# A graph-attention kernel whose second layer is normalized after its product instead of before

## The chip, the cores and the metric

The kernel runs on one core of a Trainium2 chip. The metric is the time of one execution on the device in microseconds; lower is better. A profile of one execution shows what each engine of the core did: TensorE (PE, with its weight loads as PEld), VectorE (DVE), ScalarE (ACT), GpSimd (POOL) and SyncE (SP), and the transfers (DMA) that SP and POOL issue.

## The reference

Two graph-attention layers are applied to 32 independent graphs of 512 nodes, and their result is added to the input. For each graph:

```python
h = maximum(layernorm(x), 0)                       # x: [512, 512]
h = elu(gat_layer(h, mask, W1, as1, ad1, b1))      # 4 heads of 256, concatenated: [512, 1024]
h = gat_layer(h, mask, W2, as2, ad2, b2)           # 1 head of 512
out = x + h

def gat_layer(x, mask, W, a_src, a_dst, bias):
    xl = x @ W                                     # per head
    asrc, adst = xl . a_src, xl . a_dst            # one score per node and head
    e = leaky_relu(asrc[s] + adst[d], 0.2)         # [source, destination]
    e = where(mask, e, -1e9)
    attn = softmax(e, over sources s)
    return sum over s of attn[s, d] * xl[s] + bias
```

`mask` is the adjacency matrix with the diagonal set. All is in f32.

## The kernel before, in words

One batch is one graph. `B` is 32; rows are taken in `NT` = 4 blocks of 128. Every large product is a Strassen-like scheme of seven half-size products (numbered 1 to 7), whose operands are sums and differences made on VectorE beforehand, and whose results are gathered in PSUM banks and evicted by ScalarE or VectorE. Per batch there are four products: the first projection (`project1`, 55 matmuls of 258 columns), the first layer's weighted sums (`gather1`, 56 of 256 columns, in two halves of two heads), the second projection (`project2`, 56 of 257: 256 features and one score column, twice), and the second layer's weighted sums (`gather2`, 28 of 256).

The main loop (L1702 to L1759) interleaves three batches. In its iteration `i` TensorE does the first half of `gather1` of batch `i+1`, 19 steps of `project1` of batch `i+2`, the second half of `gather1` of `i+1`, the rest of `project1` of `i+2`, then `gather2` of batch `i`, then `project2` of `i+1`. Beside this, the input of batch `i+3` is loaded, normalized, and turned by `norm_turn`: ScalarE splits the f32 words into 16-bit halves, a DMA transpose on SP turns them (`x<-adj` in the profile), and ScalarE merges the halves into `ht`.

The softmax weights of one head are made by the class `Soft` in two passes. The first pass (`first`) has destinations on the partitions: for each block of 128 destinations ScalarE takes the leaky ReLU of the scores (`l<-as,z`), VectorE applies the mask and takes the least negated value (`l<-l,mt`, with the result in column block 0 of `low`), and ScalarE exponentiates and sums (`l<-l,low`, sum in column block 1 of `low`). The logarithm of that sum is subtracted from the extreme, so that `low` holds minus (maximum + log sum). `spread` broadcasts these per-destination values to all partitions by way of DRAM (`drr<-rr`, `rr<-drr`). The second pass (`second`) has sources on the partitions: VectorE makes the leaky ReLU shifted by the broadcast values, a POOL transfer adds the mask (`p<-dm`), and ScalarE exponentiates. The weights `p` come out normalized.

`gather2` multiplies `p` with the projected features `xl2`. `residual(i)` loads the four row blocks of x into four `t` tiles before it; the function `put` inside `gather2` adds every one of the 14 results from PSUM to its half of a row block on VectorE (`t<-mm,t`), and when a row block is complete SP stores it (`out_dram<-t`). The tiles `t` are also the operands `t<-p` of `gather1`.

Nothing in the order of the work outside TensorE is written out by hand. All operations are collected as jobs with an engine, an estimated cost, reads and writes. The order of TensorE's jobs is that of the program. For the other engines a planner (`Program.order`, `Run.go`) simulates the queues with its estimated costs, and `Program.better` looks for holes of TensorE in its own model; for each it tries up to `TRIES` changes of the other engines' priorities, and keeps those that help. The order found is then emitted; every engine executes its list in order.

Of the kernel before, what the change touches and what calls it, by code (L numbers as in the profile page):

```python
# [11 lines left out]
F32 = mybir.dt.float32  # L12
# [4 lines left out]
OP = mybir.AluOpType  # L17
# [186 lines left out]
class Program:  # L204
# [224 lines left out]
    MARK, SIGHT, TRIES, BACK = 20, 80, 100, 5.0  # L429
# [83 lines left out]
def tile_gat(  # L513
# [66 lines left out]
    half = sbuf.tile([P, NT], F32, name="half")  # L580
# [10 lines left out]
    c2 = sbuf.tile([P, 2], F32, name="c2")  # L591
    cols2 = sbuf.tile([P, 2, 2], F32, name="cols2")
# [11 lines left out]
    xs = slots("x", NT, [P, D])  # L604
# [5 lines left out]
    ts_ = slots("t", 4, [P, N])  # L610
# [341 lines left out]
    class Soft:  # L952


        def __init__(self, b, layer, scores):
            self.b, self.layer, self.scores = b, layer, scores
            self.g = 2 if layer == 1 else 1
            self.z, self.asr, self.low, self.rr, self.p = {}, {}, {}, {}, {}
# [46 lines left out]
        def first(self, h, parts=((0, NT),)):  # L1005
# [9 lines left out]
            for d0, d1 in parts:  # L1015
                for d in range(d0, d1):
                    lk, e = ls.take()
                    act(
# [3 lines left out]
                    e3 = e.rearrange("p (t r) -> p t r", r=P)  # L1022
# [13 lines left out]
                act(0.25, tot, tot, low[:, 1, d0:d1], low[:, 1, d0:d1], AF.Ln)  # L1036
                dve(
                    TINY, lo + tot, lo, nc.vector.tensor_sub,
                    low[:, 0, d0:d1], low[:, 0, d0:d1], low[:, 1, d0:d1],
                )  # L1040
# [129 lines left out]
    def sevens(left, right, rkeys, put, kh, units, width, order, seeds={}):  # L1170
# [3 lines left out]
        for u, n in order:  # L1174
            m = units[u][0]
            acc, first = ACC[n], n in (1, 2, 5)
# [16 lines left out]
            put(n, units[u], bk, ps)  # L1193
# [360 lines left out]
    def sums2(b, soft, place=None, keys=None):  # L1554
# [4 lines left out]
        v = x2(b)  # L1559
        b11, b12, b21, b22 = (  # L1560
            (
                v[:, 2 * r : 2 * r + 2, c * W2H : c * W2H + M],
# [5 lines left out]
            (t.rearrange("p (k f) -> p k f", f=M), [k]) for k, t in (xs.take() for _ in range(3))  # L1568
# [13 lines left out]
    def gather2(b, soft, blocks, order=NEAR):  # L1582
        left, right = blocks
        xr = XR.pop(b)
        upper = [2, 2]

        def put(n, u, bk, ps):
            r, c = BLOCK[n - 1]
            d = 2 * r + u[0]
            place, xk, xt = xr[d]  # L1590
            to = xt[:, c * M : (c + 1) * M]
            dve(ADD, [bk, xk + (c,)], [xk + (c,)], nc.vector.tensor_tensor, to, ps, to, op=OP.add)

            upper[u[0]] -= n in (2, 3)
            if n == 4 or r == 0 and upper[u[0]] == 0:
                upper[u[0]] = -1
                dma(0.65, [xk, xk + (0,), xk + (1,)], (), out[b, d * P : (d + 1) * P, :], xt)
                place.give(xk)
# [3 lines left out]
            [(0,), (1,)], M, order,  # L1602
# [31 lines left out]
    def second_layer(b):  # L1634
        s = Soft(b, 2, scores_2(b))
        s.columns(0)

# [64 lines left out]
    for i in range(B - 1):  # L1702
# [37 lines left out]
        if i < B - 3:  # L1740
            residual(i)
# [59 lines left out]
```

## Time and profile before

| | |
|---|---|
| Median of 3 runs | 2754.67 us (2753.43 to 2755.41) |
| Profiled execution, its own time | 2758.68 us |
| Its span, first to last instruction | 2756.9 us |
| Mean granted TensorE clock | 0.999 |
| Matmul instructions (two for each f32 matmul) | 12490 |
| VectorE instructions counted as busy | 6744 |
| ScalarE instructions counted as busy | 4871 |
| Issues of the mask transfer p<-dm | 314, median 4.9 us to landing |
| Loads of x into t tiles | 124 |
| Stores of t tiles | 124 |

The lines of the profile give for each engine its busy time, that time's share of the span, and its instructions. Groups of instructions are named as output<-inputs by the program's names, without buffer numbers. Since all operations are emitted by helpers, the line numbers are those of the helpers: L646 is ScalarE's `act`, L649 VectorE's `dve`, L652 SP's `dma`, L657 POOL's `accumulate`, L663 TensorE's `pe`; L932 is the transpose of x. Times in a timeline are counted from the start of the span. Matmuls overlap, so that one that takes 379 ns follows the one before it by about 216.

### The profile page before, as it was taken

What the parts mean: (1) busy time and instruction counts of PE and PEld (TensorE: products, weight loads), DVE (VectorE), ACT (ScalarE), POOL (GpSimd) and SP (SyncE); (2) the same over time, 40 slices, a digit from 0 to 9 for tenths busy, and PEclk for the clock granted to TensorE, in tenths of its full rate; (3) what the DMA queues carried; (4) which work ended last, traced back from release to release, by engine and by line L of the source; (5) the groups of instructions that cost most, each with busy time, mean ns of one, the idle gap of its engine ahead of it and who ended that gap; (6) DMA issues with size and microseconds to landing.
All of it is one profiled execution on the core that took longest, in us unless ns stands there. A gap on an engine that the chain in (4) does not pass through costs nothing.

```text
span 2756.9 us, 41901 instructions
## 1 busy us (share of the span) xinstructions
PE 2732.9 (99%) x12490; PEld 2367.0 (86%) x12490; DVE 2595.0 (94%) x6744; ACT 2281.9 (83%) x4871; POOL 326.5 (12%) x356
## 2 busy tenths in 40 slices
PE   7999999999999999999999999999999999999999
PEld 6688888888888888888888888888888888888887
DVE  8999999999999999999999999999999999999996
ACT  5978898888888888988889887888888898888973
POOL 0111110101111011111011110111111111101110
PEclk9999999999999999999999999999999999999999
DMA  8756866667676677666776666766666766777663
GB/s 225 182 162 181 206 177 173 182 182 194 174 193 176 177 184 206 179 168 183 187 207 173 182 176 183 191 188 182 178 182 180 213 173 172 185 183 199 169 169 108
DMA packets 375863, 502.10 MB, mean 182 GB/s; under 512 B 222804, under 2 KB 227668, under 8 KB 375636
## 3 DMA queue, kind: packets, MB, share of 16 engines
q1 hardware_dynamic: 329844, 332.68, 43.3%
q0 software_dynamic: 45792, 166.74, 24.7%
q8 instruction: 100, 1.64, 0.2%
q14 instruction: 127, 1.04, 0.1%
HBM read 316.41 MB, written 51.31 MB: 133 GB/s over the span
## 4 chain that ended last, share of the span: by engine, by line
PE 97%; DMA 1%; ACT 1%; DVE 0%; SPq 0%; issue 0%; ACTq 0%
PE mm L663 97%; DMA x<-adj 0%; DMA w_sb<-dm 0%; ACT l L646 0%; DMA w_sb<-in_L_gnn_W_dram 0%; DMA as<-das 0%; DMA das<-as 0%; SPq L652 0%; DVE h L649 0%; ACT x L646 0%; DVE hs L649 0%; ACT ht L646 0%; DVE w_sb L649 0%; ACT w_sb L646 0%; DVE xl L649 0%
## 5 line engine op out<-in xcount | busy, mean ns | idle before, releaser
L663 PE MATMUL mm<-w_sb,hs 128*128 128x257 f32 (+2 forms) x3032 | 696.4, 380 | 2.2 <-ACT xl L646 1.6
L663 PEld LDWEIGHTS mm<-w_sb,hs 128*128 128x128 f32 x3032 | 575.3, 190 | 87.7 <-ACT xl L646 2.4
L657 POOL DMA_DIRECT2D p<-dm x314 | 274.3, 878 | 2330.5 <-DVE p L649 1312.6
L646 ACT ACTIVATE l<-l,low 128x512 f32<-128x512 f32 x640 | 458.2, 719 | 23.1 <-DVE low L649 20.6
L663 PE MATMUL mm<-w_sb,h 128*128 128x257 f32 x2056 | 467.9, 379 | 0.0
L663 PE MATMUL mm<-p,xl 128*128 128x256 f32 (+1 forms) x1984 | 466.6, 383 | 0.0
L649 DVE SCALAR_TENSOR_TENSOR p<-rr,z 128x512 f32<-128x512 f32 (+1 forms) x636 | 453.8, 739 | 0.0
L646 ACT ACTIVATE l<-as,z 128x512 f32<-128x512 f32 x640 | 436.7, 714 | 17.4 <-DMA as<-das 16.7
L663 PEld LDWEIGHTS mm<-w_sb,h 128*128 128x128 f32 x2056 | 389.2, 189 | 58.1 <-issue 0.5
L646 ACT ACTIVATE p<-p,z 128x512 f32<-128x512 f32 (+1 forms) x636 | 422.0, 718 | 11.3 <-DVE p L649 8.4
L649 DVE CUSTOM_DVE_ANT_1 l<-l,mt 128x512 f32<-128x512 f32 x640 | 424.8, 681 | 4.4 <-ACT l L646 2.3
L663 PEld LDWEIGHTS mm<-p,xl 128*128 128x128 f32 x1984 | 377.3, 190 | 58.8 <-issue 6.9
L663 PE MATMUL mm<-w_sb,ht 128*128 128x258 f32 x1802 | 419.5, 382 | 2.9 <-ACT ht L646 2.9
L663 PEld LDWEIGHTS mm<-w_sb,ht 128*128 128x128 f32 x1802 | 340.7, 190 | 55.7 <-ACT ht L646 3.3
L646 ACT ACTIVATE h<-mm,b_sb 128x256 f32<-128x256 f32 (+1 forms) x504 | 226.2, 475 | 184.5 <-PE mm L663 183.8
L646 ACT ACTIVATE xl<-mm 128x258 f32<-128x258 f32 (+2 forms) x686 | 258.3, 380 | 84.0 <-PE mm L663 80.6
L649 DVE TENSOR_TENSOR xl<-xl,mm 128x258 f32<-128x258 f32 (+1 forms) x526 | 215.4, 416 | 51.6 <-PE mm L663 47.4
L663 PE MATMUL mm<-t,hs 128*128 128x256 f32 x992 | 226.1, 380 | 0.0
L663 PEld LDWEIGHTS mm<-t,hs 128*128 128x128 f32 x992 | 189.0, 191 | 26.1 <-DVE t L649 0.3
L649 DVE TENSOR_TENSOR t<-mm,t 128x256 f32<-128x256 f32 (+1 forms) x424 | 171.7, 417 | 15.8 <-PE mm L663 13.3
L646 ACT ACTIVATE xr<-h 128x512 f32<-128x512 f32 x256 | 157.6, 624 | 34.5 <-DVE h L649 32.9
L663 PE MATMUL mm<-xl,p 128*128 128x256 f32 (+1 forms) x752 | 179.3, 387 | 0.0
(132 smaller groups left out, 3451.2 us busy)
## 6 DMA issues: line engine op xcount, KB each, us to landing
p<-dm POOLq DMA_DIRECT2D x314, 512.0 KB, 4.9
rr<-drr SPq DMA_DIRECT2D x159, 512.0 KB
x<-in_x_dram SPq DMA_DIRECT2D x129, 256.0 KB
adj<-in_adj_dram SPq DMA_DIRECT2D x128, 256.0 KB
as<-das SPq DMA_DIRECT2D x64, 512.0 KB
t<-in_x_dram SPq DMA_DIRECT2D x124, 256.0 KB
out_dram<-t SPq DMA_DIRECT2D x124, 256.0 KB
dm<-m SPq DMA_DIRECT2D x64, 256.0 KB
```

The source lines that it names most:

```text
L646: prog.add("ACT", cost, reads, writes, lambda: nc.scalar.activation(*a, **k))
L649: prog.add("DVE", cost, reads, writes, lambda: f(*a, **k))
L657: lambda: nc.gpsimd.dma_start(to, at, accum_op=OP.add), size,
L663: f(*a, **k)
```

## The change

For the batches before the last three (`whole` is false there), the second layer's weights are no longer normalized before the product:

- The first pass takes only the extreme. VectorE applies the mask to the broadcast source scores themselves and takes the least negated value; the destination's own score and the leaky ReLU are applied to that one value per destination by two small operations. The Prelu, the exponential, its sum and the logarithm fall away.
- A memset on POOL writes ones over the two score columns of the second layer's features, once the scores have been read from them. The product takes these columns along (257 instead of 256), so that its last column is the sum of the weights.
- In `gather2` the first product is forked into a second bank when one is free, the first result of every quarter is copied by ScalarE into the `t` tile, and only later ones are added by VectorE (`row_put`). When a row block is complete (`row_end`), VectorE takes the reciprocal of the sum column, ScalarE scales the row block by it, a POOL transfer adds x from DRAM (`accumulate`), and SP stores the result. The load of x ahead of `gather2` (`residual`) falls away.
- The tiles `x` and `t` become slices of one wider tile each, some small tiles share one tile, and `TRIES` goes from 100 to 24.

```diff
-    MARK, SIGHT, TRIES, BACK = 20, 80, 100, 5.0
+    MARK, SIGHT, TRIES, BACK = 20, 80, 24, 5.0
...
+            self.whole = layer == 1 or b >= B - 3
...
+                    e3 = e.rearrange("p (t r) -> p t r", r=P)
+                    if not self.whole:
+                        dve(
+                            0.62, [ok, tk + (0,), tk + (1,)], [lk, wk + (0, d)], nc.vector.tensor_tensor_reduce,
+                            out=e3, in0=o[:, j, :].rearrange("p (t r) -> p t r", r=P), in1=mt[:, :, d, :],
+                            scale=-1.0, scalar=BIG, op0=OP.add, op1=OP.min, accum_out=low[:, 0, d : d + 1],
+                        )
+                        ls.give(lk)
+                        continue
                     act(
                         0.62, [ok, *keys], [lk], e, o[:, j, :], AF.Prelu,
...
-                act(0.25, tot, tot, low[:, 1, d0:d1], low[:, 1, d0:d1], AF.Ln)
-                dve(
-                    TINY, lo + tot, lo, nc.vector.tensor_sub,
-                    low[:, 0, d0:d1], low[:, 0, d0:d1], low[:, 1, d0:d1],
-                )
+                if self.whole:
...
+                else:
+                    dve(
+                        TINY, lo + keys, lo, nc.vector.tensor_sub,
+                        low[:, 0, d0:d1], low[:, 0, d0:d1], zj[:, d0:d1],
+                    )
+                    dve(
+                        TINY, lo, lo, nc.vector.scalar_tensor_tensor,
+                        low[:, 0, d0:d1], low[:, 0, d0:d1], SLOPE, low[:, 0, d0:d1],
+                        op0=OP.mult, op1=OP.min,
+                    )
...
-            put(n, units[u], bk, ps)
+            fork = banks.take(width, width) if n == 1 and forks else None
+            if fork:
+                bank[u, "g"] = fork
+                act(0.29, [bk], [fork[0]], fork[1][:, :width], ps, AF.Copy)
+            else:
+                put(n, units[u], bk, ps)
...
     def gather2(b, soft, blocks, order=NEAR):
         left, right = blocks
-        xr = XR.pop(b)
-        upper = [2, 2]
+        xr = XR.pop(b) if soft.whole else {}
+        w = M if soft.whole else M + 1
+        upper, fresh = [2, 2], set()
+
+        def row_put(n, u, bk, ps):
+            r, c = BLOCK[n - 1]
+            d = 2 * r + u[0]
+            if d not in xr:
+                xk, _ = ts_.take()
+                xr[d] = ts_, xk, t_wide[xk[1]].rearrange("p (c f) -> p c f", c=2)
+            place, xk, xt = xr[d]
+            to = xt[:, c]
+            if (d, c) in fresh:
+                dve(ADD, [bk, xk + (c,)], [xk + (c,)], nc.vector.tensor_tensor, to, ps, to, op=OP.add)
+            else:
+                fresh.add((d, c))
+                act(COPY, [bk, xk], [xk + (c,)], to, ps, AF.Copy)
+
+        def row_end(d):
+            place, xk, xt = xr[d]
+            halves, total, y = [xk, xk + (0,), xk + (1,)], xt[:, 0, M:w], xt[:, :, :M]
+            dve(TINY, [xk + (0,)], [xk + (0,)], nc.vector.reciprocal, total, total)
+            act(0.62, halves[1:], halves[1:], y, y, AF.Copy, scale=total)
+            rows = slice(d * P, (d + 1) * P)
+            accumulate(1.2, halves, halves, y, x[b, rows, :].rearrange("p (c f) -> p c f", c=2))
+            dma(0.65, halves, (), out[b, rows, :].rearrange("p (c f) -> p c f", c=2), y)
+            place.give(xk)
...
     def second_layer(b):
         s = Soft(b, 2, scores_2(b))
         s.columns(0)
+        if not s.whole:
+            v = x2(b)
+            keys = [x2_key(b, t, c) for t in range(NT) for c in range(2)]
+            prog.add(
+                "POOL", 0.4, (), keys,
+                lambda: nc.gpsimd.memset(
+                    bass.AP(tensor=v.tensor, offset=v.offset + M, ap=[v.ap[0], [DO + 2, NT], [W2H, 2]]), 1.0
+                ),
+            )
...
         if i < B - 3:
-            residual(i)
             run(gather2(i, S2[i], sums2(i, S2[i])))
```

## The prediction

> **What bounds the kernel now.** I read the page first (engine totals, then the chain that ended last), then the waits of TensorE, then its timeline where waits fall, then two stages cut out of one batch.
>
> ```profile
> span 2756.9 us, 41901 instructions
> ...
> PE 2732.9 (99%) x12490; PEld 2367.0 (86%) x12490; DVE 2595.0 (94%) x6744; ACT 2281.9 (83%) x4871; POOL 326.5 (12%) x356
> ...
> PE 97%; DMA 1%; ACT 1%; DVE 0%; SPq 0%; issue 0%; ACTq 0%
> ```
>
> TensorE is busy in all but 24.0 us of the span and makes 97% of the chain. VectorE is at 94% and ScalarE at 83%, but what they cost is only what TensorE waits for. The waits of TensorE (waiter, releaser, total us, times, longest):
>
> ```profile
> PE mm L663 <- ACT x L646: 12.6, 1, 12.6
> PE mm L663 <- ACT ht L646: 2.9, 1, 2.9
> PE mm L663 <- ACT w_sb L646: 1.9, 1, 1.9
> PE mm L663 <- ACT xl L646: 1.6, 1, 1.6
> PE mm L663 <- DVE h L649: 0.6, 1, 0.6
> PE mm L663 <- DVE hs L649: 0.5, 1, 0.5
> ```
>
> That is the whole list: 12.6 us is the first load of x, 2.9 the transposed input of the second batch at 46 us. Between 60 and 2670 us, some 30 batches of 84.5 us, TensorE is kept waiting twice, together 2.1 us, both in one batch at 656 us. So no work taken off VectorE or ScalarE in the middle can win more than some 2 us, and with the end (1.9 + 0.6) some 5 us, 0.2% of the time. Under about 0.2% a measurement of this kernel cannot tell a change from none.
>
> Two stages of one ordinary batch, the second layer's product (28 matmuls of 256 columns, two instructions each) and the second projection (56 of 257); the columns are the window, its length, and the engines' busy time with instruction counts:
>
> ```profile
> 1030.30:1042.40 12.10, 12.10 (x57) 10.60 (x57) 11.93 (x36) 9.09 (x25) 0.00 (x0) 1.00 0.37 131
> 1042.40:1066.80 24.40, 24.40 (x114) 21.23 (x113) 22.65 (x60) 22.43 (x47) 4.98 (x5) 1.00 0.78 204
> ```
>
> TensorE is full in both. In TensorE's timeline these stages begin at 1030.33, 1042.42 and 1066.77 us, so an instruction takes 12.09/56 = 0.2159 us at 256 columns and 24.35/112 = 0.2174 us at 257.
>
> **A rule of the skill beside the trace.** The Trainium skill, "TensorE: Matmul & The Clock Gate", section "Back-to-back issue gap", gives a warm matmul N/2.4 + 2.5 ns. Here a 512-column instruction has a mean of 593 ns and a 256-column one 379, so a column costs 0.83 ns, which is the rule's slope only if an f32 instruction streams each column twice. The forecast goes by the trace. Part 1 of the same page, on the clock gate, says that after a pause the array runs at half rate until it has been busy some 3.4 us. The timeline of TensorE shows that after the hole at 2672 us:
>
> ```profile
> 2671.11 1.03 PE L663 MATMUL mm<-p,hs 128*128 128x256 f32 x4
> 2674.06 1.47 PE L663 MATMUL mm<-w_sb,xl 128*128 128x256 f32 x4 [1.92 <-ACT w_sb L646]
> 2675.32 1.91 PE L663 MATMUL mm<-p,xl 128*128 128x256 f32 x4
> 2677.03 1.75 PE L663 MATMUL mm<-t,hs 128*128 128x256 f32 x4
> 2678.62 1.03 PE L663 MATMUL mm<-w_sb,xl 128*128 128x256 f32 x4
> ```
>
> Four instructions should advance by 0.86 us; from 2674.06 to 2678.62 twelve advance by 4.56 instead of 2.59, so the slow clock added 2.0 us to a hole of 1.9. At 656 us, two holes of 0.5 and 1.6 us left no slow stretch behind them. A longer hole is thus paid about one and a half times over, a short one once.
>
> **The change, part by part.** It touches 29 of 32 batches (the last three keep the old way), 116 row blocks.
>
> TensorE: each of 28 x 2 x 29 = 1,624 instructions gets one column more. At 0.83 ns that is 1.35 us; at the difference of the two stages above, 1.5 ns, 2.4 us. Nothing hides it. I take 1.9.
>
> ScalarE loses, per batch, four Prelus (0.714 us), four exponentials (0.719) with their sums read out (0.196) and a logarithm (0.202): 6.7 us. It gains two copies within PSUM (nearest row 0.374), eight evictions (nearest, 257 columns, 0.376) and four scalings of 128x512 by a column (between 0.62, an exponential with a fixed scale, and 0.80, the ReLU with a column as scale; I take 0.72): 6.6 us. The total stays; its place moves. The work removed lay in the stages before the second layer's product; the work added lies in it and just behind. There ScalarE had 12.1 - 9.1 = 3.0 us free and gets 3.8, and in the stage after it 2.0 us free and gets 2.9. So some 1.7 us slips to the stage behind, where the transposed input of the next batch is put together (ht, at the end of `norm_turn`). The scalings wait for VectorE's reciprocals, and behind them stand the evictions of the second projection; eight PSUM banks and a 2.0 us margin in that stage cover a late reciprocal, and without them each 0.1 us late would be 0.1 us on TensorE.
>
> VectorE loses 10 of 14 additions from PSUM (0.414): 4.1 us. It gains four reciprocals of one column and one small operation (rows of that size take 0.15): 0.8 us. The first-pass reductions stay at 0.68 us, and the subtractions grow by two elements of 512. Net -3.4 us a batch, -97 in all, and TensorE waits for VectorE 1.1 us in the whole run: worth 0 to 1.1 us.
>
> Queues: SP loses four loads (0.37 us to issue), POOL gains four accumulating transfers (0.88 each by the mask's row; up to twice that, since each row is now two pieces) and a memset. POOL is 12% busy, so its time is free. Its waits are not: a row's transfer waits for ScalarE's scaling, and the mask transfers of the next heads stand behind it; those exponentials waited for masks only 2.9 us in all. On SP a row's store, released before by an addition, now waits for a landing (median 4.9 us for a mask of twice the size). The bytes are the same. Behind the stores stand the row broadcasts (`drr<-rr`, `rr<-drr`) and the transposes `x<-adj`.
>
> **Where I expect a new wait.** The chain of transposes is the tight one. In the batch above, the last merge ends 2.3 us before the projection that reads it starts (ScalarE's line, then TensorE's):
>
> ```profile
> 1075.15 1.37 ACT L646 ACTIVATE ht<-x 128x1024 uint16<-128x1024 uint16 x1
> ```
>
> ```profile
> 1078.86 2.34 PE L663 MATMUL mm<-w_sb,ht 128*128 128x258 f32 x10
> ```
>
> When one transpose took 9.2 us at 645 us (the longest piece of DMA in the chain of that stretch), TensorE waited. The instruction lists of the two kernels as built show how the order moves (the search for an order also gets 24 tries per hole in place of 100). On SP the four stores, spread before, now stand in one row ahead of the transposes in 25 of 29 batches. In one batch, the 24th counted from 1, ScalarE's list has the merges of the last two row blocks behind the evictions of the first two products of the same projection, and SP's list has the second pair of transposes behind a broadcast load. That wait is forced by the order. From the projection's start: the second product ends at 1.74 us, its eviction at about 2.2, an exponential 0.6, two merges of 1.2 and 1.4, a sum on VectorE 0.7, signals 0.1: 6.2 us. TensorE has work up to 2.18 (two products and one small one). Hole 4.1 us, and slow clock 2.2 (2.0 after the hole of 1.9): 6.3 us, near 1930 us of the span. Its bounds are 3 (the exponential is early, no slow clock) and 8.
>
> In a few other batches the last merge is listed directly ahead of the first eviction, with no spare place; I put 0 to 3 us on these, 1.4 as the likely. The wait of 656 us may or may not come again, since that transpose was late by chance of traffic: -2.1 or 0; I take -1.0. Start and end are listed in another order too, without a reason for a sign: plus or minus 2.
>
> **Sum.** +1.9 (columns) + 6.3 (the forced wait) + 1.4 - 1.0 - 0.5 (VectorE) = +8.1 us on the profiled execution, whose span was 2756.9 us and whose own time was 2758.68, 1.8 us around it. The median of the runs shown is 2754.67, 4.0 below that execution, and the difference carries over: 2762.8. I round down to 2762, as a wait planned by hand from a list is likelier over- than underrated.
>
> **Rivals.** (a) The columns alone, not slower by more than can be told: in the one batch with the late merges TensorE has been held up a little already and the two evictions come early, so that the hole stays below 2 us and leaves no slow stretch. For it speaks that only two waits are seen in 30 batches now. It gives 1.9 - 1.0 + 0 to 1.5 us, 2755 to 2757. It decides if that hole is under some 2 us. (b) Stores hold up SP: the accumulating transfers land late (over 5 us) in most batches, the transposes behind the four stores come 3 us later, the 2.3 us of slack is gone, and TensorE waits 0.7 to 1 us in 15 to 25 batches: +10 to +25 us, 2767 to 2782. Against it: in the batch above the last stores went out at 1056.6 us and the transposes at 1059 to 1069, so there is time between. (c) Faster: the order found with a less loaded VectorE closes the hole at 656 and those at the end, and the forced wait is filled: 2.1 + 2.5 - 1.9 gives -2.7 us at best, 2752; over 0.2% would need a shorter start as well. (d) The change does not do what it says: the lists as built do show 116 accumulating transfers and 257 columns, so this is out.
>
> **Numbers.** My forecast 0.50, (a) with partly filled waits 0.32, (b) 0.13, (c) 0.05. The forecast's own range is 2758 to 2767; part of its low side lies within 0.2% (below 2760.2). Slower 0.57, within 0.2% 0.40, faster 0.03. The range for 8 in 10 reaches from (a) into the low half of (b): 2755 to 2770.
>
> **What would show it.** Right: instructions at 217 ns in the second layer's product; TensorE's waits with a new one on ht or hs of 3 us or more near 1930 us with a slow stretch behind it; VectorE near 2500 us busy, ScalarE near 2280; no wait of TensorE on a t row. Wrong: no wait in that batch (then a), waits of TensorE on ht in many batches with transposes landing late (then b), or a pitch that stays at 216 ns.

## The result, and the profile after

The changed kernel takes 2803.85 us (median of 4 runs, 2790.39 to 2806.70) against 2754.05 us before (4 runs, 2753.25 to 2755.41): a ratio of 1.0166, 95% interval [1.0144, 1.0189]. It is 50 us slower, where 8 were forecast. The page of the changed kernel (engine totals, DMA queues, the chain that ended last by engine). Its helpers stand five lines lower: L651 is ScalarE, L654 VectorE, L657 SP, L662 POOL's transfers, L668 TensorE, L937 the transpose of x; `x` and `t` appear as `x_all` and `t_all`. A queue's line gives packets, megabytes and share of the DMA engines; q0 carries POOL's transfers (166.74 MB before), q1 those of SP (332.68 MB before).

```profile
span 2800.9 us, 41929 instructions
...
PE 2749.5 (98%) x12490; PEld 2364.1 (84%) x12490; DVE 2524.7 (90%) x6597; ACT 2287.8 (82%) x4902; POOL 461.1 (16%) x501
...
q1 hardware_dynamic: 327988, 302.27, 41.1%
q0 software_dynamic: 77344, 197.16, 31.9%
...
PE 87%; DMA 5%; DVE 4%; ACT 4%; issue 1%; SPq 0%; POOL 0%; DVEq 0%; POOLq 0%; ACTq 0%
```

The engine totals are near the forecast: VectorE lighter by 70 us (97 forecast), ScalarE the same, TensorE's instruction count the same. Some 30 MB, the 116 row blocks of x, have moved from q1 to q0. What the forecast did not have is the last line: DMA had 1% of the chain before and has 5%. TensorE's list of waits (waiter, releaser, total us, times, longest):

```profile
PE mm L668 <- DVE hs L654: 13.1, 6, 10.4
PE mm L668 <- ACT x_all L651: 11.9, 2, 11.7
PE mm L668 <- ACT p L651: 9.7, 2, 6.2
PE mm L668 <- ACT mm L651: 4.9, 5, 2.8
PE mm L668 <- DVE t_all L654: 1.8, 2, 1.3
```

The load of x at the start (`x_all`) was there before. New are 13.1 us on `hs`, the sums of the transposed input `ht`, and 9.7 us on `p`, the attention weights. From the starts of TensorE's instructions, counting as lost whatever exceeds their usual spacing (holes, and the slow stretches behind them), I get 14.9 us lost before and 55.6 after. Three places of the changed kernel make 31.8 of it: 1751 us (10.4), 1946 us (13.0) and 2115 us (8.4). The 40.7 us more, with 1.7 for the wider columns (below), account for 42.4 of the 44.0 us between the two profiled executions (2802.64 and 2758.68 us).

Neither `hs` nor `p` is the origin. These are the waits of ScalarE for mask transfers and for transposes, before and after:

```profile
ACT ht L646 <- DMA x<-adj: 5.6, 3, 3.3
ACT p L646 <- DMA p<-dm: 2.9, 4, 1.7
```

```profile
ACT p L651 <- DMA p<-dm: 33.1, 22, 6.5
ACT adj L651 <- DMA x_all<-adj: 8.6, 2, 8.2
ACT ht L651 <- DMA x_all<-adj: 2.0, 1, 2.0
```

8.5 us became 43.7. `p<-dm` is the accumulating mask transfer on POOL's queue, `x<-adj` the transpose of the next input on SP's. The change edits neither. Their own lines (POOL's accumulating transfers with the time from issue to landing, then the time SP needs to issue a transpose; min/median/max) of before and after:

```profile
L657 POOL DMA_DIRECT2D p<-dm x314: 862/862/1466, 65.3 to 2712.0; - x157
...
DMA to landing us min/median/max: 4.1/4.9/9.9
```

```profile
L662 POOL DMA_DIRECT2D p<-dm x314: 857/865/2033, 61.1 to 2755.7; - x157
...
DMA to landing us min/median/max: 4.2/6.7/18.3
```

```profile
L932 SPq DMA_TRANSPOSE x<-adj x120: 1231/1260/2480, 80.3 to 2591.8; - x120
```

```profile
L937 SPq DMA_TRANSPOSE x_all<-adj x120: 1231/1310/5862, 105.3 to 2637.7; - x120
```

The issue of a mask transfer costs POOL what it did. Its landing takes 6.7 us instead of 4.9 in the median (both kinds of transfer together after; by its mask transfers alone it is 6.7 as well), and 27 of 314 mask transfers land after more than 9 us, where 3 did. A transpose, which SP used to issue in 2.5 us at most, can take 5.9. Here is the largest hole, by the chain that ended last in this stretch (start, us, what):

```profile
1937.43 0.01 POOLq L662
1937.45 14.54 DMA p<-dm
1951.99 0.02 issue
1952.02 0.72 ACT p L651
1952.74 0.27 ACT xl L651
1953.01 0.61 ACT p L651
1953.62 2.42 ACT ht L651 x2
1956.04 0.02 issue
1956.07 0.70 DVE hs L654
```

and by SP's and TensorE's timelines around it:

```profile
1928.52 3.00 SPq L937 DMA_TRANSPOSE x_all<-adj  x2
...
1935.13 7.01 SPq L937 DMA_TRANSPOSE x_all<-adj  x2
```

```profile
1944.04 2.34 PE L668 MATMUL mm<-w_sb,ht 128*128 128x258 f32 x10
1956.82 3.81 PE L668 MATMUL mm<-w_sb,hs 128*128 128x258 f32 x8 [10.44 <-DVE hs L654]
```

A mask transfer is issued at 1937.45, in the middle of the second pair of transposes, whose issue stretches to 7.0 us. In the same batch before, the second pair went out 12.8 us ahead of the next mask transfer (SP and POOL before, then POOL after):

```profile
1910.73 2.64 SPq L932 DMA_TRANSPOSE x<-adj  x2
```

```profile
1923.52 0.86 POOL L657 DMA_DIRECT2D p<-dm  x1 [19.54 <-DVE p L649]
```

```profile
1934.92 0.86 POOL L662 DMA_DIRECT2D p<-dm  x1 [1.89 <-DVE p L654]
1937.45 0.86 POOL L662 DMA_DIRECT2D p<-dm  x1 [1.66 <-PE mm L668]
```

The mask of 1937.45 lands 14.5 us later. Two exponentials on ScalarE need it, and ScalarE's list has the last two merges of `ht` behind them; the sum `hs` follows, and TensorE has stood for 10.4 us. At 1743 us the same chain has `DMA p<-dm` with 18.3 us, at 2103 us `DMA x_all<-adj` with 15.3 us.

Counted over the whole trace, all six mask transfers that took more than 12 us had a transpose being issued while they were in flight. The 47 that met only x transfers took 8.4 us in the median and 11.2 at most; the 140 that met neither, 5.9 and 11.8. So in this trace x transfers in flight go with a longer landing, and the longest landings go with transposes. The x transfers themselves were over by then: the last of the batch had landed at 1921.34, 16 us ahead of the mask of 1937.45, and at 1741.08 and 2102.41 in the other two places.

How this fits into a batch is seen best from the start of the second projection (medians over some 30 batches, us, from the starts and landings in the trace):

| | before | part three alone | after |
|---|---|---|---|
| last x transfer issued / landed | – | 2.4 / 12.2 | 4.6 / 13.7 |
| third mask transfer issued / landed | 11.2 / 16.1 | 12.3 / 19.6 | 13.7 / 20.7 |
| fourth mask transfer issued / landed | 14.2 / 19.5 | 15.3 / 22.4 | 15.6 / 23.2 |
| last store issued | 16.7 | 12.3 | 13.8 |
| first transpose issued | 17.5 | 17.7 | 17.3 |
| third transpose's source copied | 23.7 | 24.9 | 26.4 |
| last transpose issued, longest | 27.8, 29.5 | 28.7, 31.4 | 29.2, 40.5 |
| first projection begins | 36.4 | | |

Before, the masks have mostly landed when the transposes go out at 17.5. After, the last of them are in flight until 23 us, beside the first two transposes. There are two `adj` tiles, so the third block is copied only when the first transpose has landed, and what the first pair loses the second pair loses too. The prediction measured 2.3 us of slack at the end of this chain. 1.4 of it is gone in the median, and in five batches the last transpose goes out after 30.5 us, once at 40.5.

### The profile page after: what moved, and what is told of

Its sections match the earlier page's. It is cut to its first block, busy times and chain, and to the rows that moved or that the text cites. A ratio compares the mean times of both kernels' runs of the same rounds, so it can differ in the third digit from the quotient of the medians.

```text
span 2800.9 us, 41929 instructions
## 1 busy us (share of the span) xinstructions
PE 2749.5 (98%) x12490; PEld 2364.1 (84%) x12490; DVE 2524.7 (90%) x6597; ACT 2287.8 (82%) x4902; POOL 461.1 (16%) x501
## 4 chain that ended last, share of the span: by engine, by line
PE 87%; DMA 5%; DVE 4%; ACT 4%; issue 1%; SPq 0%; POOL 0%; DVEq 0%; POOLq 0%; ACTq 0%
PE mm L668 87%; DMA p<-dm 2%; ACT l L651 1%; DVE p L654 1%; DMA x_all<-adj 1%; ACT p L651 1%; DVE l L654 1%; DVE hs L654 0%; DVE h L654 0%; DMA rr<-drr 0%; DMA out_dram<-t_all 0%; ACT adj L651 0%; ACT xl L651 0%; DVE t_all L654 0%; DVE w_sb L654 0%
## 5 line engine op out<-in xcount | busy, mean ns | idle before, releaser
L668 PE MATMUL mm<-w_sb,hs 128*128 128x257 f32 (+2 forms) x3032 | 698.4, 381 | 13.0 <-DVE hs L654 12.5
L668 PEld LDWEIGHTS mm<-w_sb,hs 128*128 128x128 f32 x3032 | 575.1, 190 | 101.4 <-DVE hs L654 15.1
L662 POOL DMA_DIRECT2D p<-dm x314 | 290.9, 934 | 1201.6 <-DVE p L654 554.1
L668 PE MATMUL mm<-p,xl 128*128 128x256 f32 (+1 forms) x1984 | 468.3, 384 | 9.9 <-ACT p L651 9.7
L668 PE MATMUL mm<-w_sb,h 128*128 128x257 f32 x2056 | 467.9, 379 | 0.0
L651 ACT ACTIVATE p<-p,z 128x512 f32<-128x512 f32 (+1 forms) x636 | 428.0, 716 | 46.4 <-DMA p<-dm 33.1
L654 DVE SCALAR_TENSOR_TENSOR p<-rr,z 128x512 f32<-128x512 f32 (+1 forms) x636 | 454.5, 745 | 5.5 <-DMA rr<-drr 5.5
L668 PEld LDWEIGHTS mm<-w_sb,h 128*128 128x128 f32 x2056 | 389.3, 189 | 58.1 <-issue 0.2
L668 PEld LDWEIGHTS mm<-p,xl 128*128 128x128 f32 x1984 | 377.3, 190 | 70.6 <-ACT p L651 11.2
L668 PE MATMUL mm<-w_sb,ht 128*128 128x258 f32 x1802 | 420.6, 382 | 2.0 <-DVE xl L654 1.6
L668 PEld LDWEIGHTS mm<-w_sb,ht 128*128 128x128 f32 x1802 | 339.0, 190 | 58.1 <-DVE xl L654 8.2
L651 ACT ACTIVATE xl<-mm 128x258 f32<-128x258 f32 (+2 forms) x686 | 259.5, 382 | 156.2 <-PE mm L668 152.6
L654 DVE CUSTOM_DVE_ANT_1 l<-l,mt 128x512 f32<-128x512 f32 x524 | 349.1, 687 | 34.8 <-ACT l L651 33.4
L651 ACT ACTIVATE l<-l,low 128x512 f32<-128x512 f32 x524 | 375.6, 719 | 4.0 <-DVE low L654 3.1
L651 ACT ACTIVATE l<-as,z 128x512 f32<-128x512 f32 x524 | 362.7, 718 | 12.7 <-DMA as<-das 12.4
L651 ACT ACTIVATE h<-mm,b_sb 128x256 f32<-128x256 f32 (+1 forms) x504 | 228.0, 478 | 137.2 <-PE mm L668 136.5
L654 DVE TENSOR_TENSOR xl<-xl,mm 128x258 f32<-128x258 f32 (+1 forms) x526 | 216.3, 422 | 61.4 <-PE mm L668 53.7
L662 POOL DMA_DIRECT2D t_all<-in_x_dram x116 | 131.0, 1283 | 713.4 <-ACT t_all L651 437.8
L668 PE MATMUL mm<-t_all,hs 128*128 128x256 f32 x992 | 232.2, 384 | 7.5 <-ACT mm L651 4.7
L668 PEld LDWEIGHTS mm<-t_all,hs 128*128 128x128 f32 x992 | 188.7, 192 | 39.9 <-ACT mm L651 8.5
L651 ACT ACTIVATE xr<-h 128x512 f32<-128x512 f32 x256 | 160.7, 633 | 51.9 <-DVE h L654 49.6
L668 PE MATMUL mm<-xl,p 128*128 128x257 f32 (+2 forms) x752 | 180.2, 388 | 0.2 <-issue 0.2
```

Of the source, the lines that this page charges most:

```text
L651: prog.add("ACT", cost, reads, writes, lambda: nc.scalar.activation(*a, **k))
L654: prog.add("DVE", cost, reads, writes, lambda: f(*a, **k))
L662: lambda: nc.gpsimd.dma_start(to, at, accum_op=OP.add), size,
L668: f(*a, **k)
```

## The experiments

All runs in one table: device time, ratio to the kernel before on the same chip, issue of the last transpose counted as above, and ScalarE's waits for mask transfers and for transposes added up.

| kernel | us | ratio, interval | last transpose, median / longest | ScalarE waits, us |
|---|---|---|---|---|
| before | 2754.05 | – | 27.8 / 29.5 | 8.5 |
| before, 24 tries | 2761.11 | 1.0019 [1.0011, 1.0026] | 27.8 / 29.9 | 14.7 |
| before, x loads estimated at 0.4 | 2763.68 | 1.0037 [1.0023, 1.0052] | 27.8 / 30.4 | 9.3 |
| change without x | 2762.57 | 1.0025 [1.0016, 1.0034] | 27.9 / 30.5 | 13.3 |
| change without x, 100 tries | 2763.15 | 1.0033 [1.0022, 1.0043] | 27.9 / 29.9 | 14.3 |
| part three alone | 2771.36 | 1.0056 [1.0039, 1.0074] | 28.7 / 31.4 | 22.8 |
| part three alone, estimate 1.8 | 2800.91 | 1.0189 [1.0158, 1.0220] | 30.4 / 36.9 | 12.6 |
| part three alone, estimate 0.6 | 2833.57 | 1.0289 [1.0262, 1.0316] | 30.0 / 38.2 | 73.1 |
| after | 2803.85 | 1.0166 [1.0144, 1.0189] | 29.2 / 40.5 | 43.7 |
| after, 100 tries | 2807.28 | 1.0199 [1.0160, 1.0238] | 29.2 / 37.1 | 38.0 |
| after, 2 KB rows | 2801.05 | 1.0168 [1.0153, 1.0183] | 29.2 / 36.0 | 41.4 |
| after, ones by VectorE | 2816.51 | 1.0218 [1.0201, 1.0236] | 29.1 / 36.9 | 42.7 |
| after, estimate 0.6 | 2836.24 | 1.0298 [1.0256, 1.0340] | 29.0 / 40.0 | 90.7 |
| after, estimate 1.8 | 2874.04 | 1.0439 [1.0403, 1.0475] | 30.7 / 37.1 | 31.2 |
| after, rows unscaled | 2860.51 | 1.0387 [1.0365, 1.0408] | 29.8 / 34.6 | 46.0 |
| after, scaling of 8 columns | 2805.36 | 1.0185 [1.0160, 1.0209] | 29.3 / 37.3 | 40.0 |
| after, third adj tile | 2780.47 | 1.0095 [1.0080, 1.0110] | 28.9 / 37.4 | 23.0 |
| after, x transfers of 8 columns | 2787.97 | 1.0105 [1.0074, 1.0137] | 29.2 / 35.2 | 34.1 |
| after, masks of 8 columns | 2769.21 | 1.0050 [1.0035, 1.0065] | 29.1 / 31.6 | 0 |
| after, both of 8 columns | 2766.89 | 1.0048 [1.0032, 1.0065] | 29.1 / 30.6 | 0 |

**The length of the search.** The change also cuts the tries for an order from 100 to 24. The kernel before with 24, and the changed kernel with 100:

```
-    MARK, SIGHT, TRIES, BACK = 20, 80, 100, 5.0
+    MARK, SIGHT, TRIES, BACK = 20, 80, 24, 5.0
```

> The kernel before with 24 tries per hole instead of 100, nothing else. If the weaker search for an order is the cause of the loss, this is slower by a good part of the 50 us: 2775 us or more. If the transfers that add x are the cause, the search alone costs 0 to 5 us: 2754 to 2760.

> The changed kernel with 100 tries per hole instead of 24, nothing else. If the search is the cause: 2770 us or less. If the transfers are: 2785 to 2810, as the changed kernel, and other batches than those at 1750, 1946 and 2115 us have the large waits.

The shorter search costs the kernel before 5 us, and the longer one gives the changed kernel nothing: 2807.28 us, with a hole of 12.1 us on `hs` again near 1940 us. The search does not explain the loss.

**The weight of the x transfers.** All instructions and their order stay, but x is added to 8 columns only; in the other run the scaled row is written in one piece, so that x and the store move rows of 2 KB.

```
-            accumulate(1.2, halves, halves, y, x[b, rows, :].rearrange("p (c f) -> p c f", c=2))
+            accumulate(1.2, halves, halves, y[:, 0, :8], x[b, rows, :8])
```

```
+            line = t_wide[xk[1]][:, : 2 * M]
...
-            accumulate(1.2, halves, halves, y, x[b, rows, :].rearrange("p (c f) -> p c f", c=2))
-            dma(0.65, halves, (), out[b, rows, :].rearrange("p (c f) -> p c f", c=2), y)
+            accumulate(1.2, halves, halves, line, x[b, rows, :])
+            dma(0.65, halves, (), out[b, rows, :], line)
```

> The changed kernel with every instruction list unchanged, but each transfer that adds x moves only 8 columns of a row block (the rest of x is not added). If the weight of these transfers delays the mask transfers and the transposes: mask landing back to some 5 us, none over 12, and 2758 to 2768 us, with the one wait near 1930 us that the order forces (4 to 6 us) left over. If the order alone is the cause: 2795 us or more.

> The changed kernel with each scaled row block written as one piece of 512, so that the transfers that add x, and the stores, move rows of 2 KB instead of twice 1 KB; same order of jobs. If the number of pieces is what weighs: the issue on POOL falls from 1.1 to 0.87 us, landing from 6.9 to some 5 us, and the time to 2765 to 2785. If bytes weigh or the order does: 2795 to 2806.

The bytes of x are worth some 16 us, a third of the loss; the ends of the two intervals allow 2 to 32. Neither expectation was met, and the time lies between them. The pieces are worth nothing that can be told. With x nearly weightless the wait on `hs` is as long as ever, so the largest hole does not come from the weight of x:

```profile
PE mm L668 <- DVE hs L654: 15.0, 5, 11.1
```

**Part three alone, and the change without it.** First the normalized weights and 256 columns of the kernel before with the x transfers of the change (and its forks and copies on ScalarE, so it is not the x transfers alone); then the change without any x transfer (x is left out of the output).

```
-            self.whole = layer == 1 or b >= B - 3
+            self.whole = True
...
-            dve(TINY, [xk + (0,)], [xk + (0,)], nc.vector.reciprocal, total, total)
-            act(0.62, halves[1:], halves[1:], y, y, AF.Copy, scale=total)
```

```
-            accumulate(1.2, halves, halves, y, x[b, rows, :].rearrange("p (c f) -> p c f", c=2))
```

> Only the third part of the change: the weights stay normalized (first pass and 256 columns as before, no memset, no reciprocal, no scaling), but the results are copied by ScalarE where they are the first of their quarter, x is added by a POOL transfer, and the store waits for it; 24 tries. If moving x to POOL's queue is the cause: 2785 us or more, with mask landings over 9 us in 20 or more cases. If the unnormalized product is: 2758 to 2768.

> The first two parts without the third: the changed kernel without the transfer that adds x (x is left out of the result); the scaled row block is stored at once; the planner knows it. If the transfers on POOL's queue are the cause: 2757 to 2768 us, mask landings near those of before (median 5, none over 13). If the work moved onto ScalarE around the second layer's product is: 2780 or more with mask landings as before.

Part three alone costs 16 us, the change without x some 8, all three parts 50. Part three alone has even more late masks than the change, 34 over 9 us against 27, but none over 11.9 us: 32 of them met x transfers. Either the parts act on each other, or 2771 is the accident of one order. The next runs were meant to tell.

**The planner's estimate, and the ones.** The estimate of an x transfer is raised to 1.8 us; separately the ones are written by VectorE, which takes the memset out of POOL's list.

```
-            accumulate(1.2, halves, halves, y, x[b, rows, :].rearrange("p (c f) -> p c f", c=2))
+            accumulate(1.8, halves, halves, y, x[b, rows, :].rearrange("p (c f) -> p c f", c=2))
```

> The changed kernel with the planner's estimate for a transfer that adds x raised from 1.2 to 1.8; the transfers are the same, only the order is another. If the loss comes from an order that counts on too light transfers: 2770 to 2790 us with fewer masks in flight while a transpose is issued (118 in the changed kernel, 64 before). If the queues cannot hold this work in any order: 2795 or more.

> The changed kernel with the ones written by VectorE instead of POOL, so that no mask transfer stands behind a memset that waits for the scores. If that wait on POOL's queue is what delays the masks near 646 and 1946 us: 2775 us or less. If not: 2790 to 2810.

An estimate nearer to the measured landing makes it worse, by 70 us, although fewer masks have a transpose issued while they are in flight (81, against 118 in the change). The planner then puts the transposes later itself: the first goes out at 20.2 us of the batch instead of 17.3, and `hs` is waited for in 16 places:

```profile
PE mm L668 <- DVE hs L654: 50.1, 16, 11.0
```

Without the memset on POOL the time is 2816.51. This run has another order too, so it gives no sign that the memset holds POOL up, and no proof that it does not. I then tried the opposite estimate, the change without x under the long search, and two runs on what the theory now was:

```
-            accumulate(1.2, halves, halves, y, x[b, rows, :].rearrange("p (c f) -> p c f", c=2))
+            accumulate(0.6, halves, halves, y, x[b, rows, :].rearrange("p (c f) -> p c f", c=2))
```

> The changed kernel with one number changed: the planner's estimate of an x transfer, 1.2 us, is set to 0.6; every transfer still moves the same bytes. With 1.8 the time was 2874 us. Theory A (the planner keeps its estimated POOL transfers and the transposes on SP apart on a common DMA account, so that a larger estimate moves the last pair of transposes of the next input later): 2785 us or less, with the last transpose earlier than 29.2 us after the start of the second projection. Theory B (the order of issue hardly matters, the transfers delay each other whenever they are in flight together): 2795 us or more. A sum outside both, 2785 to 2795, tells nothing.

> The changed kernel without the x transfers (x is left out of the output, each row goes to its store as soon as it is scaled), and with the search of 100 tries of the kernel before. With 24 tries this took 2762.6 us. Theory A (the first two parts of the change cost the 2 us of the wider columns and nothing else, and the rest of those 7.8 us is the shorter search): 2755 to 2759 us. Theory B (the scaled rows and the maximum pass cost TensorE waits of their own): 2761 us or more.

Both of my favoured theories failed. The low estimate gives 2836.24 us: the transposes are issued earlier (the first at 15.8 us) and meet the mask transfers more often; 46 of these take over 9 us, and ScalarE waits 90.7 us. So both ends are bad, one by order, the other by collision. And the long search does not bring the change without x below 2763.15 us, so its 8 us are not the search's.

**The weight of the mask transfers.** The order and every instruction list of the changed kernel, but each mask transfer moves 8 of 1,024 columns:

```
-                            *(t[:, us[0] : us[-1] + 1].rearrange("p t n -> p (t n)") for t in (p, md)),
+                            *(t[:, us[0], :8] for t in (p, md)),
...
-                        0.62 if long else 0.36, keys + [zk + (2,)], keys, p[:, u, at], p[:, u, at], AF.Exp,
-                        bias=z[:, 2, j, u : u + 1],
+                        0.62 if long else 0.36, keys + [zk + (2,)], keys, p[:, u, at], p[:, u, at],
+                        **(dict(func=AF.Exp, bias=z[:, 2, j, u : u + 1]) if self.layer == 2 else dict(func=AF.Relu, scale=1e-4)),
```

> The changed kernel with every mask transfer cut to 8 of its 1,024 columns per partition; the exponential of the first layer's weights becomes a Relu with a scale of the same size, so that nothing overflows. The instruction lists, and the order on every queue, are those of the changed kernel; the mask and the weights are left out of the result. Theory A (mask transfers of 512 KB in flight beside the transposes make both late, and that is what opens the holes of TensorE): 2768 us or less, and no hole over 3 us near 1946 us. Theory B (the order of issue alone makes the transposes late, whatever the transfers move): 2795 us or more, with the hole near 1946 us still there.

2769.21 us: 35 of the 50 us are gone, although I had asked for 2768 and for a hole below 3 us. The holes at 1751 and 2115 us have vanished, and the one near 1946 (here near 1930) is down from 10.4 us to 3.7:

```profile
1919.44 3.38 SPq L937 DMA_TRANSPOSE x_all<-adj  x2
```

```profile
1927.85 2.34 PE L668 MATMUL mm<-w_sb,ht 128*128 128x258 f32 x10
1933.92 3.81 PE L668 MATMUL mm<-w_sb,hs 128*128 128x258 f32 x8 [3.73 <-DVE hs L654]
```

The same pair of transposes is issued in 3.4 us instead of 7.0. One thing besides the bytes changes here: the Relu takes 621 ns where the exponentials take some 716, which takes ScalarE from 2287.8 to 2242.2 us, 0.1 us at each step; that cannot fill a hole of 6.7 us, but may be a small part of the 35 (22 to 42 by the ends of the intervals). What the run shows is that the masks' bytes cost this much under this order. It does not part their own late landing, for which ScalarE waited 33.1 us, from the delay of the transposes, 10.6 us of its waits; no run made the transposes light. Later the transfers of x were cut as well:

> The changed kernel's order and instruction lists with both kinds of POOL transfers cut to 8 columns per partition (mask, weights and x are left out of the result as in the two runs before). x cut alone gave 2788 us, the mask alone 2769. Theory A (all that is left beyond the 2 us of columns is weight in flight): 2755 to 2762 us, and the last transposes at 28.2 us or less after the start of the second projection in the median. Theory B (the order itself holds the last transposes 1.3 us back and keeps costing): 2765 to 2772 us, with the median still at 29.0 us or more.

2766.89 us. Once the masks are light, the x transfers weigh nothing that can be told (2 us, inside the intervals). With full masks they were worth some 16, which suggests that they do their harm through the masks and transposes that they run into. The median of the last transposes stays at 29.1 us with every transfer light, so that this 1.3 us comes with the order, not with weight; weight makes the tail, 40.5 us against 30.6. What is left of the order is the hole that the prediction had named:

```profile
PE mm L668 <- DVE hs L654: 5.3, 4, 3.7
```

**The row chain.** If the copy, reciprocal and scaling of a row start its x transfer later, and so push the masks behind it into the transposes, then a shorter chain should help. First without reciprocal and scaling (x added to the unnormalized row), then, since that gave the planner other costs, with the scaling cut to 8 columns under unchanged costs:

```
-            dve(TINY, [xk + (0,)], [xk + (0,)], nc.vector.reciprocal, total, total)
-            act(0.62, halves[1:], halves[1:], y, y, AF.Copy, scale=total)
```

```
-            act(0.62, halves[1:], halves[1:], y, y, AF.Copy, scale=total)
+            act(0.62, halves[1:], halves[1:], y[:, :, :4], y[:, :, :4], AF.Copy, scale=total)
```

> The changed kernel without the reciprocal and without the scaling of a row: x is added to the unnormalized row as soon as its last merge is done. The part three alone took 2771 us, the first two parts without x 2762.6, all three 2802. Theory A (the interaction is that the longer row chain of part one, 0.9 us of ScalarE and VectorE work ahead of each x transfer, starts the x transfers later and so pushes the mask transfers behind them into the transposes): 2765 to 2778 us. Theory B (the interaction lies elsewhere, in the copies and forks of the product or in the order that the planner finds): 2795 us or more.

> The changed kernel, its order and all its instructions, with the scaling of a finished row cut from 512 to 8 columns per row (the rest of the row stays unscaled); unlike the earlier run without scaling, the planner sees the same costs. Each x transfer can start about 0.5 us earlier. Theory A (the longer row chain is what pushes the mask transfers into the transposes): the third mask transfer is issued 13.0 us or less after the start of the second projection instead of 13.7, and the time is 2785 us or less. Theory B (the chain's length is not the lever, the order on the queues is): 2795 to 2810 us.

The theory falls. Without the scaling the third mask goes out at 12.1 us as hoped, but the new order issues the second transpose at 21.0 us, 0.6 later than the changed kernel, and the time is 2860.51. With the order kept, the last x transfer starts at 3.7 us instead of 4.6, yet the third mask moves only from 13.7 to 13.5, and the time does not move: 2805.36. The traces show what holds that mask: it goes out 0.3 us after VectorE's operation on `p` (the leaky ReLU to which it is added), in the median of all nine runs in which this was counted, and that operation ends at 11.0 us before, at 13.4 in the change and at 13.2 here. The place of VectorE's work in the order sets the issue of the mask, not the x transfers ahead of it on POOL's queue.

**A third adj tile.** So that the third block need not wait for the first transpose to land (one xr tile is given up for the room):

```
-    adjs = slots("adj", 2, [P, N], I32)
-    xrs = slots("xr", 3, [P, N])
+    adjs = slots("adj", 3, [P, N], I32)
+    xrs = slots("xr", 2, [P, N])
```

> The changed kernel with a third adj tile (and two xr tiles instead of three, for the room), so that the third of an input's four transposes need not wait until the first has landed. All transfers stay. Theory A (TensorE's holes come from the last pair of transposes being issued after 30 us from the start of the second projection, because the pair waits for the landing of the first): the last transposes are issued at 28 us or earlier in the median, and the time is 2780 us or less. Theory B (the transposes are held up in flight by the mask transfers, all four together, and an earlier issue meets them as well): 2790 us or more.

2780.47 us, 23 less than the change. The third block is now copied at 22.9 us instead of 26.4, but the fourth at 27.7 (27.8 in the change), and the last transpose goes out at 28.9 rather than at the 28 I had asked for. The edit brings another order with it, and the next runs show that orders alone differ by more than 23 us; so it is no proof for the tiles.

**Interaction, or the order?** Part three alone with estimates of 0.6 and 1.8, and the kernel before with a halved estimate of its own loads of x:

```
-            dma(0.8, [x2_key(b, 0, 0)], halves, xr, x[b, d * P : (d + 1) * P, :])
+            dma(0.4, [x2_key(b, 0, 0)], halves, xr, x[b, d * P : (d + 1) * P, :])
```

> Part three alone (normalized weights, 256 columns, copies on ScalarE, x added by POOL transfers; 24 tries), with the planner's estimate of an x transfer set from 1.2 to 0.6 us; the bytes stay. With 1.2 it took 2771 us. In the full change the same edit moved 2802 to 2836 us. Theory A (part three alone keeps some 1.3 us of slack ahead of the first projection in any order, and the first two parts use it up): 2765 to 2780 us. Theory B (any order that holds x transfers scatters by tens of us, and part three alone met a good one): 2785 us or more.

> Part three alone with the planner's estimate of an x transfer at 1.8 us (1.2 gave 2771 us, 0.6 gave 2834). Theory A (any other order that holds the x transfers loses tens of us, and 2771 was a favourable order): 2790 us or more. Theory B (only the low estimate is bad, since it lets the planner set the transposes too near to the transfers): 2763 to 2780 us.

> The kernel before with the planner's estimate of one plain load of a block of x rows on SP, which is 0.8 us, set to 0.4; the bytes stay. A halved estimate of the x transfers on POOL moved part three alone from 2771 to 2834 us and the whole change from 2802 to 2836. Theory A (a new order costs tens of us only where x goes through POOL's queue ahead of the mask transfers): 2752 to 2765 us, and no mask transfer lands after more than 13 us. Theory B (any new order scatters as widely, and the order of the kernel before is a lucky one): 2775 us or more.

Part three alone takes 2833.57 and 2800.91 us in these orders. The low estimate shows the collision, in ScalarE's waits:

```profile
ACT adj L651 <- DMA x_all<-adj: 36.3, 9, 7.1
...
ACT p L651 <- DMA p<-dm: 25.8, 20, 4.5
```

The high one shows late planning: hardly a wait of ScalarE, but the first transpose at 20.6 us and the last at 30.4. The kernel before in a new order takes 2763.68, and no mask of it lands later than 10.3 us. So no interaction between the parts is needed to explain the 50 us, though none is excluded: 2771 was a favourable order. The five kernels without x on POOL lie between 2754 and 2764 us; the eleven with full transfers of x and masks and two adj tiles lie between 2771 and 2874.

## Why the prediction was wrong

*TensorE bounds the kernel, and the columns cost 1.9 us.* Right. In TensorE's timeline the second layer's product of one batch runs from 1033.28 to the first instruction of the projection at 1045.43, 12.15 us for 56 instructions, 0.2170 us each. Against the 12.09 of before that is 0.06 us in a batch, 1.7 us in 29.

```profile
1033.28 1.90 PE L668 MATMUL mm<-xl,p 128*128 128x257 f32 x8
...
1045.43 4.95 PE L668 MATMUL mm<-w_sb,h 128*128 128x257 f32 x22
```

*ScalarE's total stays, VectorE's falls by 97 us.* ScalarE 2281.9 to 2287.8, right. VectorE fell by 70, in part because each operation takes about 1% longer in this profile (687 ns for a first-pass reduction, 681 before); as neither engine was the bound, the difference costs nothing.

*The forced wait in the 24th batch.* Right, and of the right size as far as the order goes: 4.1 us of hole and 2.2 of slow clock were forecast near 1930 us; with light masks the hole is 3.7 us and the whole loss there 6.6, with both light 3.7 and 4.0. So a slow stretch behind a hole is no fixed price: the eight instructions behind the one hole took 3.81 us, and behind the other, equally long, 2.01. The order without the weight costs 14.3 us (8.8 to 17.9 by the interval of the ratio) where the sum said 8.1; the 1.4 us for other tight batches was too small, since between 170 and 2200 us the kernel with both light loses some 9 us outside that hole, in places of 0.1 to 2.4 us, where the kernel before lost 3. In the changed kernel itself the hole was 10.4 us. The step that failed there is "an exponential 0.6": I counted the exponential that stands ahead of the merges, and not the mask transfer that it waits for. It landed 14.5 us after its issue.

*"POOL is 12% busy, so its time is free", "those exponentials waited for masks only 2.9 us in all", "The bytes are the same."* This is the step that sank the forecast. All three are true of what they count: POOL ends at 16%, and a mask transfer still issues in 0.86 us. But the wait of before stood in for the wait after, so that the sum has no term for later masks; that wait grew from 2.9 to 33.1 us. The bytes of x moved from SP's loads, spread over the batch, to four transfers in 4 us just ahead of the mask transfers on POOL's queue. The last of them lands 9 us after its issue, the masks beside them land later, VectorE's place in the new order sends the third mask out 2.5 us later as well, and the last masks are then in flight beside the transposes on SP. The Trainium skill, "DMA: Bandwidth & Descriptors", section "Issuing engines are not separate DMA queues", says that transfers started by different engines run on the same 16 DMA engines and interleave. The trace agrees: the light masks let SP issue the same pair of transposes in 3.4 us instead of 7.0. The page gives no price for this; here the masks' bytes cost 35 us under this order, which bounds the price of the meeting and does not measure it alone. The program itself held a price: in `SHARED` its planner lets the transfers of SP and POOL run at 0.44 and 0.62 of their speed when both queues have one in flight, and at 0.22 and 0.45 when SP's is a transpose. These are estimates in the program, not measurements, but the forecast could have started from them. I had costed a queue by its issuing engine, and a transfer by its bytes, and never by what else is in flight then.

*Rival (b), stores hold up SP.* It had the place (transposes late, slack of 2.3 us gone) and too small a price, 10 to 25 us, but its mechanism is not what happened. The last store goes out at 13.8 us of a batch, earlier than before (16.7), and the first transpose at 17.3 against 17.5. My objection to it, that there is time between stores and transposes, was right; I took it for an objection to late transposes as such. Nor is it 0.7 to 1 us in 15 to 25 batches: 31.8 us were lost in three. In two of these three (1743 and 2103 us) the transposes followed the last store at once, at 15.4 and 13.2 us of the batch instead of 17.3; they went out early there, while the masks were in flight.

*The chances.* No case of mine reached beyond 2782 us, since every delay I could think of was a median delay set against the slack. A chain that has 2.3 us to spare, on transfers with a landing between 4 and 18 us, is decided by the tail.

What stays open: why the planner puts VectorE's operation on `p` 2.4 us later, and which orders let the masks meet the transposes, could not be read from the change. How much of the 35 us is this meeting, and how much the late masks by themselves, no run here shows.

## What to carry to other kernels

Cost a transfer that moves to another queue by what is in flight when it and those queued behind it run, not by the issuing engine's idle time: here part three alone, which moves bytes without adding any, cost 16 us in one order and 81 in another. When a listed instruction stands ahead of a critical one on its engine, follow its inputs too, down to the DMA that releases it, and set the slack against the longest landing in the trace and not against the median. Where a planner orders the work, run the edit under two or three estimates before saying what it is worth; its order alone moved this edit from 2771 to 2834 us, while the kernel before, with no such transfers, stayed within 11 us.

## What the runs showed of the hardware

Accumulating transfers of 512 KB issued by POOL landed in 4.9 us in the median and 9.9 at most before the change, where 64 of the 314 had a transpose issued while they were in flight; after it 118 had, and the longest took 18.3 us. The transposes are held up in turn: an issue on SP, 1.26 us in the median and 2.48 at most before, took up to 5.86, and 2.64 at most with light masks under the same order. I had not expected the issue itself to stretch. Cut to 8 columns, the same mask transfers still took 2.6 us in the median, so roughly half of the 4.9 us of before is not the bytes. Rows in pieces of 1 KB or of 2 KB made no difference that could be told (2803.85 and 2801.05 us).
